# Gates beside the convolution's tanh in one visit of tables, two preparation steps a state up to the ninth, and sums of states from the fourth on

## The chip, the cores and the metric

The kernel runs on one core of a Trainium2 chip. The metric is the device time of one execution in microseconds (us). "Before" is the kernel as it stands; "after" has the change.

The core's engines are named as the profile names them: PE (TensorE, matrix products), DVE (VectorE), ACT (ScalarE, activation functions from a loaded table), POOL (GpSimd) and SP (SyncE, which here issues DMAs). PEld is TensorE's weight load.

## The reference

The input `x` is 8 batches of 256 tokens with 128 features. Three blocks follow each other, each with a residual and a layernorm: a state-space block (the one that is changed), a cross-attention to a context, and six layers of local attention with a feed-forward network. The state-space block, cut to what matters:

```python
Xn      = layernorm(X) * ln_g + ln_b
X_main  = silu(causal_depthwise_conv(Xn @ W_up1.T, taps=4) + conv_b)   # 256 channels
pp      = X_main @ W_ll.T + b_ll
delta   = softplus(pp[..., :256]);  Bm = pp[..., 256:272];  Cm = pp[..., 272:288]
A       = -exp(A_log)                                     # 256 channels x 16 states
dA      = delta[..., None] * A
A_bar   = exp(dA)
U       = X_main[..., None] * (A_bar - 1) / dA * (delta[..., None] * Bm[:, :, None, :])
H_t     = A_bar_t * H_{t-1} + U_t                         # a scan over the 256 tokens
Y_t     = sum over the 16 states of C_t * H_t
out     = X + (Y * silu(Xn @ W_up2.T)) @ W_down.T + b_down
x       = layernorm(x + out)
```

## The kernel before

**Stages.** The state-space stage takes the first 374 us of some 2310, then come cross-attention and the six layers. The stage works on four pairs of batches, `p` = 0 to 3. A tile is 128 partitions (channels or features) by 512 columns (the 256 tokens of two batches). The 256 channels are two halves, `h` = 0 and 1.

**Three generators per pair.** `pre(p)` prepares a pair: it loads and transposes `x`, makes the layernorm (`xn`), the convolution as four matmuls a half (L370, tile `conv`), then silu of it as half x times (1 + tanh) (`xm`: a tanh and an Identity on ACT, L94 and L383, a multiplication on DVE). From `xm` a matmul makes B and C (`bc_ps`, L389), which ACT copies to `bc` and stores in DRAM (L398). `minus_bc` makes `cb`, the product of B and C. `step_of` and `softplus` make `dt`, the step, for each half: an Abs, a Relu (`z`, L418, one buffer), an exp, an Ln, and an addition (on POOL for pairs 1 to 3, L424). At last the gate: two matmuls (`g_ps`), a tanh each (`gate`, L94), and a multiplication on DVE (L467).

`scan(p)` (L525) walks the 16 states. For each state SP issues two DMAs that spread a row of B and a row of C over 128 partitions (`rows`, four buffers), and for each half, a "half-state":

- `wz` = `xm` x a constant x row of B, on DVE (L538), a ring of four tiles;
- `dw`, its difference between neighbouring tokens, on POOL (L544);
- `ab` = exp(`dt` x A), on ACT (L94 `ab`), in PSUM;
- `m`, two scans over 256 tokens, on DVE (L519);
- `mc` = `m` x row of C, on POOL (L521), six buffers;
- `add_up()`: PE adds `mc` to the sum `y[h]` in PSUM with the identity as weights (L499).

`ab`, `m` and `mc` of a half-state are issued two half-states behind its `dw`. At state 2 a small product `s_ps` (L552) and a first matmul (L555) start the two sums. `add_up()` is called at the beginning of a state, from the fifth on (`n > 3`); each call adds the `mc` that have been issued since the last, so the first call adds those of the first three states (with the lag of two half-states).

`post(p)` multiplies the sum by the gate (L478), projects it down (`dn_ps`, L483), and makes the residual and its layernorm.

**How they are interleaved.** While `scan(p)` runs, `both` alternates steps of `post(p-1)` and `pre(p+1)`; each `yield` ends a step. The number of steps a state is set at L556: none at the first state, then two up to `n <= 5`, then one; two always in pair 3. In pair 2 a further generator, `project(0)` of the cross-attention (matmuls `pr`, L242, and a layernorm with its own Ln), is stepped once a state from `n > 5`; in pair 3 it takes the place of `pre`.

**Tables.** ACT's exp and Ln come from one set of tables, its tanh from another (which has exp too). `load_table` switches (`ACT_TABLE_LOAD`, L102) and keeps the program's order; `with_table` holds an activation behind the load that is issued last, and `behind_exps` holds it behind the exp that is issued last. In `pre` there are two visits to the tanh's set, each with a load there and a load back: one for `xm` (L378 to L386), one for the gate (L462 to L469).

**Order of the instructions.** Apart from the first eight steps of `pre(0)`, which are ordered by hand, a scheduler of the framework orders each engine's instructions in this stage within these limits. PSUM tiles with the tag "s" (convolution, `bc_ps`, `d_ps`, `g_ps`, `s_ps`, `dn_ps`, `pr` and others) share a ring of two.

Of the kernel before, what the change touches and what calls it, by code (L numbers as in the profile page):

```python
# [9 lines left out]
FP = mybir.dt.float32  # L10
AF = mybir.ActivationFunctionType
ALU = mybir.AluOpType
AX = mybir.AxisListType

P = 128
B, S, D = 8, 256, 128
NPAIR = B // 2
TP = 2 * S
# [31 lines left out]
def decoder_kernel(ctx: ExitStack, tc: tile.TileContext, a: dict, out: bass.AP):  # L50
# [14 lines left out]
    def ps_s(name):  # L65
        return banks[-1].tile([P, 512], FP, tag="s", name=name)
# [31 lines left out]
    def load_table(name="natural_log_exp_and_others"):  # L98

        late = name == "exp_and_others" and logs  # L100
        with tc.issue_after(logs[-1].ins) if late else ExitStack():
            table.append(tc.keep_in_program_order(A.preload_act_table_set(name)))  # L102
# [166 lines left out]
    with (  # L269
# [76 lines left out]
        def behind_exps():  # L346

            return tc.issue_after(exps[-1].ins) if exps else ExitStack()

        def pre(p, got, t_in=None):  # L350


            x = new_x(p)
            t_in = t_in or load_x(p)
            yield
            tp = turned_tokens(t_in)
            yield
            A.copy(x, tp)
            layernorm_tokens(t_in, on_act=p > 0)
            yield  # L360
            tp = turned_tokens(t_in)
            yield
            xn = xns[p % 2][:, :, KC - 1 :]
            A.activation(xn, two(tp), AF.Identity, bias=col("ssm_b"), scale=col("ssm_g"))
            xm, gate, dt, acc = [], [], [], []
            got.update(x=x, xm=xm, gate=gate, dt=dt)
            for h in range(2):
                acc.append(ps_s("conv"))
                for k in range(KC):
                    T.matmul(  # L370
                        acc[h], lhsT=w_tap[:, h, k, :],
                        rhs=xns[p % 2][:, :, k : k + S], start=(k == 0), stop=(k == KC - 1),
                    )
                yield

            for _ in range(2 if p else 0):
                yield
            load_table("exp_and_others")  # L378
            for h in range(2):
                m = sp.tile([P, TP], FP, tag=f"xm{h}", name="xm")  # L380
                with behind_exps():
                    with_table(A.activation, m, acc[h], AF.Tanh, bias=half_b[:, h : h + 1])
                A.activation(m, m, AF.Identity, bias=1.0)  # L383
                V.scalar_tensor_tensor(m, acc[h], half_b[:, h : h + 1], m, ALU.add, ALU.mult)
                xm.append(m)
            load_table()  # L386
            bc_ps = ps_s("bc_ps")
            for k in range(2):
                T.matmul(  # L389
                    bc_ps[: 2 * NS], lhsT=w_ll[:, k, DI:], rhs=xm[k], start=(k == 0), stop=(k == 1)  # L390
                )
            yield
            bc_sb = sp.tile([2 * NS, TP], FP, name="bc", bufs=1)
            with behind_exps():
                A.activation(bc_sb, bc_ps[: 2 * NS], AF.Identity, bias=col("b_bc", 0, 2 * NS))

            bc = dp.tile([2 * NS, TP], FP, name="bc_dram")
            nc.scalar.dma_start(out=bc, in_=bc_sb)  # L398
            cb = sp.tile([NS, TP], FP, name="cb", bufs=1)
            got.update(bc=bc, cb=cb, b_ps=[])  # L400

            def step_of(h):
                d_ps = ps_s("d_ps")
                for k in range(2):
                    T.matmul(
                        d_ps, lhsT=w_ll[:, k, h * P : (h + 1) * P], rhs=xm[k],
                        start=(k == 0), stop=(k == 1),
                    )
                return d_ps

            def softplus(h, d_ps):

                e = sp.tile([P, TP], FP, name="ez")
                with behind_exps():
                    A.activation(e, d_ps, AF.Abs, bias=col("b_dt", h))
                z = sp.tile([P, TP], FP, name="z", bufs=1)
                if p:
                    A.activation(z, d_ps, AF.Relu, bias=col("b_dt", h))  # L418
                else:
                    V.tensor_scalar(z, d_ps, col("b_dt", h), 0.0, ALU.add, ALU.max)  # L420
                with_table(A.activation, e, e, AF.Exp, scale=-1.0)
                logs.append(with_table(A.activation, e, e, AF.Ln, bias=1.0))
                t = sp.tile([P, TP], FP, tag=f"dt{h}", name="dt")
                (G if p else V).tensor_tensor(t, z, e, ALU.add)  # L424
                dt.append(t)

            def minus_bc():

                c_ps = ps_s("c_ps")
                T.matmul(  # L430
                    c_ps[:NS], lhsT=ident[: 2 * NS, NS : 2 * NS], rhs=bc_sb, start=True, stop=True
                )
                V.scalar_tensor_tensor(cb, c_ps[:NS], -1.0, bc_sb[:NS], ALU.mult, ALU.mult)

            if p:
                minus_bc()
                for h in range(2):
                    d_ps = step_of(h)
                    yield
                    softplus(h, d_ps)  # L440
                yield
            else:

                for h in range(2):
                    d_ps = step_of(h)
                    t = ps1.tile([P, TP], FP, tag="ab", name="b_ps")
                    T.matmul(
                        t, lhsT=ident[: 2 * NS, h : h + 1].to_broadcast([2 * NS, P]), rhs=bc_sb,
                        start=True, stop=True,
                    )  # L450
                    got["b_ps"].append(t)
                    softplus(h, d_ps)
                yield
                minus_bc()
            g_ps = []
            for h in range(2):
                g_ps.append(ps_s("g_ps"))
                T.matmul(
                    g_ps[h], lhsT=w_up2[:, h * P : (h + 1) * P], rhs=xn, start=True, stop=True
                )  # L460
            yield
            load_table("exp_and_others")  # L462
            for h in range(2):
                g = sp.tile([P, TP], FP, tag=f"gate{h}", name="gate")
                with behind_exps():
                    with_table(A.activation, g, g_ps[h], AF.Tanh)
                V.scalar_tensor_tensor(g, g, 1.0, g_ps[h], ALU.add, ALU.mult)  # L467
                gate.append(g)
            load_table()  # L469

        def post(p, x, gate, y):

# [18 lines left out]
        def scan(p, x, xm, gate, dt, bc, b_ps, cb, steps, spare):  # L491
# [31 lines left out]

            waiting = []
            for n in range(NS):  # L525
                if n > 3:
                    add_up()

                rows = sp.tile([P, 2, TP], FP, name="rows", bufs=4)
                early = n < len(b_ps)  # L530
                for i in range(1 if early else 0, 2):
                    r = i * NS + n
                    nc.sync.dma_start(out=rows[:, i, :], in_=bc[r : r + 1, :].to_broadcast([P, TP]))
                for h in range(2):
                    c = h * NS + n
                    w = wzs.pop(0)
                    wzs.append(w)
                    V.scalar_tensor_tensor(  # L538
                        w[:, :, 1:], two((xm if n < 2 else xp1)[h]), ia[:, c : c + 1],
                        two(b_ps[n] if early else rows[:, 0, :]),  # L540
                        ALU.mult, ALU.mult,
                    )
                    dw = sp.tile([P, TP], FP, name="dw", bufs=3)
                    G.tensor_tensor(two(dw), w[:, :, 1:], w[:, :, :S], ALU.subtract)  # L544
                    waiting.append((h, n, dw, rows))

                    if len(waiting) > 2:
                        scan_of(*waiting.pop(0))
                if n == 2:
                    for h in range(2):  # L550
                        s_ps = ps_s("s_ps")
                        T.matmul(s_ps, lhsT=iaT[:, h, :], rhs=cb, start=True, stop=True)  # L552
                        t = sp.tile([P, TP], FP, tag=f"yg{h}", name="xs1")
                        V.tensor_tensor(t, xm[h], s_ps, ALU.mult)
                        T.matmul(y[h], lhsT=ident, rhs=t, start=True, stop=False)  # L555
                for _ in range(0 if n == 0 else 2 if n <= 5 or p == NPAIR - 1 else 1):  # L556
                    next(steps, None)
                if n > 5:
                    next(spare, None)
# [702 lines left out]
```

## Time and profile before

| | |
|---|---|
| median of 3 runs | 2314.65 us (2313.25 to 2314.94) |
| the profiled execution | 2312.42 us, span 2310.3 us, mean granted TensorE clock 0.974 |
| busy over the whole span | PE 2150.0 (93%), DVE 1786.0 (77%), POOL 1646.2 (71%), ACT 1492.1 (65%) |
| end of the state-space stage | last `mc` starts at 372.48 us |
| table loads in the first 350 us | 17, 1283 ns each |
| `mc` (POOL L521), whole stage | 128, 1277 ns each; POOL idle ahead of them 39.5 us |

All times in views are microseconds from the start of the profiled span, unless marked ns. In a timeline, a row gives start, duration, engine, line, operation, and in brackets the idle time before it with what ended it. In the row of a group, the count is followed by busy time, mean duration in ns, and the idle time just before them with its releasers.

### The profile page before, as it was taken

How to read it: one execution, taken by the hardware profiler on the slowest of the kernel's cores; microseconds unless marked ns; L12 is line 12 of the kernel's file. 1: busy time of each engine (PE TensorE's matmuls, PEld its weight loads, DVE VectorE, ACT ScalarE, POOL GpSimd, SP SyncE). 2: the span in 40 equal slices, each digit the busy share in tenths (PEclk: the TensorE clock that was granted, in tenths of full speed). 3: DMA queues.
4: the chain of work that ended last, by engine and by line, in shares of the span. 5: the costliest groups of instructions: out<-in, count | busy, mean ns of one | idle time of the engine just before them, and what ended most of it. 6: DMA issues, size and time to landing. Idle time of an engine off the chain costs nothing.

```text
span 2310.3 us, 52806 instructions
## 1 busy us (share of the span) xinstructions
PE 2150.0 (93%) x20194; PEld 1339.5 (58%) x20194; DVE 1786.0 (77%) x2558; ACT 1492.1 (65%) x2505; POOL 1646.2 (71%) x1437
## 2 busy tenths in 40 slices
PE   7776888999988999999999999999999999999986
PEld 3232333444446666666666666666666666666664
DVE  6798876454558888888888888888888888888873
ACT  5544544455556776776777676777776776777664
POOL 4888876232478878777787777787877777777760
PEclk8888889999999999999999999999999999999999
DMA  4343331000213334333343334343343334333331
GB/s 139 96 106 98 95 88 39 2 4 1 86 26 56 65 59 90 69 70 60 70 81 71 69 63 88 67 73 62 63 85 71 72 61 76 62 63 61 56 66 32
DMA packets 438229, 153.84 MB, mean 67 GB/s; under 512 B 401887, under 2 KB 418141, under 8 KB 437853
## 3 DMA queue, kind: packets, MB, share of 16 engines
q1 hardware_dynamic: 437500, 150.10, 32.9%
q8 instruction: 162, 2.65, 0.5%
q14 instruction: 87, 0.70, 0.1%
q10 hardware_dynamic: 480, 0.38, 0.1%
HBM read 54.68 MB, written 1.31 MB: 24 GB/s over the span
## 4 chain that ended last, share of the span: by engine, by line
PE 33%; DVE 21%; ACT 21%; POOL 11%; issue 6%; DMA 1%; POOLq 0%; ACTq 0%; SPq 0%; DVEq 0%
DVE rb L700 5%; DVE qk L699 4%; PE qk_ps L682 4%; ACT sq L705 4%; ACT kz L751 3%; POOL pw L800 3%; PE f_ps L919 3%; POOL qk L703 3%; ACT pw L94 3%; PE qkT_ps L738 3%; PE o_ps L833 2%; DVE ss L712 2%; PE pr L242 2%; PE y_ps L852 2%; PE v_ps L682 2%
## 5 line engine op out<-in xcount | busy, mean ns | idle before, releaser
L703 POOL TENSOR_TENSOR qk<-qk,rb 128x512 f32<-128x512 f32 x384 | 484.7, 1284 | 108.5 <-DVE rb L700 88.7
L731 POOL TENSOR_TENSOR qk<-qk,rn 128x1024 f32<-128x1024 f32 x192 | 366.7, 1910 | 133.9 <-ACT rn L94 109.4
L682 PE MATMUL qk_ps<-wqkv,xs 128*128 128x512 f32 x768 | 364.7, 597 | 2.7 <-ACT sq L705 2.6
L705 ACT ACTIVATE sq<-qk_ps 128x1024 f32<-128x1024 f32 x192 | 196.8, 1025 | 180.5 <-DVE rb L700 170.5
L699 DVE TENSOR_TENSOR qk<-qk_ps,tab 128x1024 f32<-128x1024 f32 x192 | 233.3, 1215 | 79.9 <-PE qk_ps L682 79.1
L800 POOL TENSOR_TENSOR pw<-pw,mx 128x512 f32<-128x512 f32 x192 | 200.5, 1044 | 91.8 <-DVE mx L799 87.1
L712 DVE TENSOR_REDUCE ss<-sq 128x16 f32<-128x1024 f32 x192 | 232.5, 1211 | 40.2 <-ACT sq L705 37.4
L700 DVE TENSOR_TENSOR rb<-qk_ps,tab 128x1024 f32<-128x1024 f32 x192 | 233.2, 1214 | 0.0
L738 PE MATMUL qkT_ps<-ident,qk 128*128 128x128 f32 x1536 | 209.0, 279 | 16.1 <-ACT v L725 10.7
L94 ACT ACTIVATE pw<-pw 128x512 f32<-128x512 f32 x192 | 120.6, 628 | 155.9 <-POOL pw L800 155.6
L751 ACT COPY kz<-qkT_ps 64x1024 f32<-64x1024 f32 x192 | 193.1, 1006 | 34.5 <-PE qkT_ps L738 32.8
L833 PE MATMUL o_ps<-vz,pT 128*32 128x128 f32 x6144 | 207.5, 276 | 8.2 <-ACT pT L825 8.2
L814 POOL TENSOR_TENSOR pw<-pw,mx 128x512 f32<-128x512 f32 x192 | 200.9, 1047 | 19.5 <-DVE mx L813 17.9
L812 DVE TENSOR_REDUCE mx<-pw 128x8 f32<-128x512 f32 x192 | 130.6, 680 | 106.2 <-ACT pw L94 105.8
L852 PEld LDWEIGHTS y_ps<-oT,wo 128*128 128x128 f32 x1536 | 186.3, 192 | 44.7 <-issue 36.8
L833 PEld LDWEIGHTS o_ps<-vz,pT 128*32 128x32 f32 x6144 | 156.0, 109 | 91.8 <-ACT rn L94 35.6
L1085 POOL TENSOR_TENSOR ws<-w 128x512 f32<-128x512 f32 x64 | 81.4, 1272 | 175.3 <-ACT w L94 162.6
L786 PE MATMUL s_ps<-kz,qT 128*32 128x128 f32 x6144 | 203.0, 273 | 0.0
L682 PE MATMUL v_ps<-wqkv,xs 128*128 128x512 f32 x384 | 185.3, 605 | 16.6 <-ACT kz L751 16.6
L738 PEld LDWEIGHTS qkT_ps<-ident,qk 128*128 128x128 f32 x1536 | 164.9, 141 | 56.3 <-issue 44.2
L521 POOL TENSOR_TENSOR mc<-m,rows 128x512 f32<-128x512 f32 x128 | 162.9, 1277 | 39.5 <-PE y L499 19.8
L682 PEld LDWEIGHTS qk_ps<-wqkv,xs 128*128 128x128 f32 x768 | 131.3, 191 | 97.9 <-issue 92.7
(186 smaller groups left out, 4224.4 us busy)
## 6 DMA issues: line engine op xcount, KB each, us to landing
vz<-v SPq DMA_DIRECT2D x1152, 64.0 KB, 2.2
rows<-bc_dram SPq DMA_DIRECT2D x126, 256.0 KB, 3.8
vz<-v SPq DMA_DIRECT2D x576, 32.0 KB, 2.3
wqkv<-in_L_ffn_Wqkv SPq DMA_DIRECT2D x18, 512.0 KB, 4.3
wo<-in_L_ffn_Wo SPq DMA_DIRECT2D x48, 64.0 KB, 2.1
w<-in_L_ffn_W SPq DMA_DIRECT2D x6, 341.0 KB, 3.5
t_in<-in_x SPq DMA_DIRECT2D x4, 256.0 KB, 3.6
wkv<-in_L_xattn_Wkv SPq DMA_DIRECT2D x1, 1024.0 KB, 7.8
```

What stands on the lines that cost most here:

```text
L682: T.matmul(pr[:, i * 512 : (i + 1) * 512], lhsT=got[n]["xs"][:, tb * P : (tb + 1) * P], rhs=thirds[seq[n][0], c][:, i * 512 : (i + 1) * 51 ...
L699: V.tensor_tensor(t, p3, cs, ALU.mult)
L700: V.tensor_tensor(rb, p3, sn, ALU.mult)
L703: G.tensor_tensor(t[:, :, o], t[:, :, o], rb[:, :, f], ALU.add)
L705: A.activation(sq, p3, AF.Square)
L712: V.tensor_reduce(got[n]["ss"][:, 2 * c + tb, :], got[n]["sq"], AX.X, ALU.add)
L731: G.tensor_tensor(t, t, r, ALU.mult)
L738: T.transpose(t_ps[:, hb * P : (hb + 1) * P], t[:, 2 * hb : 2 * hb + 2, :].rearrange("p h d -> p (h d)"), ident,)
L751: A.copy(fixed3["kzs"][0][r, :, e, W + tb * P : W + (tb + 1) * P], t3[r])
L800: G.tensor_tensor(pw, pw, mx[:, 0].unsqueeze(3).to_broadcast(shape), ALU.subtract)
L833: T.matmul(o_ps[i * W : (i + 1) * W, j * P : (j + 1) * P], lhsT=pT[:, j, i * W : (i + 1) * W], rhs=vz[:, j, i].rearrange("p e d -> p (e d) ...
L852: T.matmul(y_ps[:, :P], lhsT=wts[d][0][:, hb, :], rhs=got[n]["oT", wh][:, hb, :], start=(hb == 0), stop=(hb == NHB - 1),)
```

## The change

For pairs 1 to 3 the load back after the convolution's tanh is left out; the gate's matmuls, tanh and multiplications follow `bc` within the same visit, ahead of `minus_bc`, the steps and softplus, and one load back ends it. For pair 0 the order stays. The sums are issued from the fourth state on (`n > 2`) in place of the fifth. Two steps a state are taken up to `n <= 8` in place of `n <= 5`.

```diff
                 xm.append(m)
-            load_table()
+            if not p:
+                load_table()
             bc_ps = ps_s("bc_ps")
...
             got.update(bc=bc, cb=cb, b_ps=[])
+
+            def gates():
+                g_ps = []
+                for h in range(2):
+                    g_ps.append(ps_s("g_ps"))
+                    T.matmul(
+                        g_ps[h], lhsT=w_up2[:, h * P : (h + 1) * P], rhs=xn, start=True, stop=True
+                    )
+                yield
+                if not p:
+                    load_table("exp_and_others")
+                for h in range(2):
+                    g = sp.tile([P, TP], FP, tag=f"gate{h}", name="gate")
+                    with behind_exps():
+                        with_table(A.activation, g, g_ps[h], AF.Tanh)
+                    V.scalar_tensor_tensor(g, g, 1.0, g_ps[h], ALU.add, ALU.mult)
+                    gate.append(g)
+                load_table()
...
             if p:
+                yield from gates()
                 minus_bc()
                 for h in range(2):
                     d_ps = step_of(h)
                     yield
                     softplus(h, d_ps)
                 yield
             else:
...
                 minus_bc()
-            g_ps = []
...
-            load_table()
+                yield from gates()
...
             for n in range(NS):
-                if n > 3:
+                if n > 2:
                     add_up()
...
-                for _ in range(0 if n == 0 else 2 if n <= 5 or p == NPAIR - 1 else 1):
+                for _ in range(0 if n == 0 else 2 if n <= 8 or p == NPAIR - 1 else 1):
                     next(steps, None)
```

More of the change, by code (lines that the diff above doesn't have):

```diff
@@ L454, in pre @@
                 minus_bc()
-            g_ps = []
[L456 to L468, printed above, removed]
-            load_table()
+                yield from gates()
         def post(p, x, gate, y):
```

## The prediction

> **What bounds the kernel now.** I read first the forty slices, because the change touches only the state-space stage (the first 375 of 2310 us, six and a half slices), then busy time by stretch, one stretch for each pair of batches.
>
> In the slices, GpSimd (POOL) is as full as the others over the first seven:
>
> ```profile
> PE   7776888999988999999999999999999999999986
> POOL 4888876232478878777787777787877777777760
> ```
>
> The stretches (pairs 0 to 3; columns: length, then busy time of PE, PEld, DVE, ACT, POOL, granted clock, DMA share, GB/s):
>
> ```profile
> 25.00:112.00 87.00, 68.99 (x127) 23.97 (x126) 71.22 (x117) 46.89 (x72) 73.17 (x65) 0.81 0.41 106
> 112.00:207.00 95.00, 69.11 (x143) 26.17 (x142) 81.02 (x138) 43.79 (x68) 82.57 (x72) 0.82 0.38 101
> 207.00:292.00 85.00, 68.68 (x158) 28.68 (x158) 75.32 (x120) 46.06 (x74) 73.83 (x65) 0.87 0.39 99
> 292.00:374.00 82.00, 61.79 (x127) 23.39 (x128) 59.87 (x96) 33.31 (x54) 68.81 (x63) 0.90 0.35 83
> ```
>
> POOL leads in every pair and ACT, whose tables the change regroups, is at half. So the ruler is POOL: a half-state costs it one `dw` (about 1.0) and one `mc` (about 1.23), back to back 2.23 us (see 64.36, 66.59, 68.81 below). A change gains only by the gaps between those. I number half-states 1 to 128, 32 a pair. POOL's long gaps, from the timeline (start, us, ..., idle before and releaser):
>
> ```profile
> 64.36 1.26 POOL L521 TENSOR_TENSOR mc<-m,rows 128x512 f32<-128x512 f32 x1 [8.29 <-PE y L499]
> 66.59 1.26 POOL L521 TENSOR_TENSOR mc<-m,rows 128x512 f32<-128x512 f32 x1
> 68.81 1.27 POOL L521 TENSOR_TENSOR mc<-m,rows 128x512 f32<-128x512 f32 x1
> ...
> 160.54 1.28 POOL L521 TENSOR_TENSOR mc<-m,rows 128x512 f32<-128x512 f32 x1 [3.70 <-PE bc_ps L389]
> 190.69 1.27 POOL L521 TENSOR_TENSOR mc<-m,rows 128x512 f32<-128x512 f32 x1 [5.40 <-PE s_ps L552]
> 245.78 1.27 POOL L521 TENSOR_TENSOR mc<-m,rows 128x512 f32<-128x512 f32 x1 [0.95 <-PE y L499]
> 276.86 1.27 POOL L521 TENSOR_TENSOR mc<-m,rows 128x512 f32<-128x512 f32 x1 [6.02 <-issue]
> 315.15 2.49 POOL L521 TENSOR_TENSOR mc<-m,rows 128x512 f32<-128x512 f32 x2 [6.36 <-PE y L499]
> ```
>
> 64.36 and 160.54 are visits to the other tables for the convolution's tanh; 190.69 and 276.86 are the separate gate visits of pairs 1 and 2; 315.15 is a wait for the sums on TensorE. The chain of waits confirms the last two (start, us, piece):
>
> ```profile
> 270.43 1.01 ACT gate L94 x2
> 271.47 1.28 ACT L102
> 272.76 1.31 ACT ab L94 x2
> ...
> 309.54 1.90 PE pr L242 x4
> 311.44 0.86 PE ln_mu L113 x2
> 312.30 1.91 PE pr L242 x4
> 314.20 0.87 PE y L499 x2
> 315.15 1.28 POOL mc L521
> ```
>
> Where the stage ends (last `mc` at 372.48, stage 2's first PE work at 374.85 right behind) moves the kernel one to one; after it both kernels issue the same order on every engine. The profiled run took 2312.42 (span 2310.3), 2.23 below the median of 2314.65. I work in its clock and add the difference to the median.
>
> **Pair 0 (preparing pair 1).** The built queues of the changed kernel hold 14 table loads in this stage against 18: two fewer in each of the preparations of pairs 1 and 2. The gate's two matmuls and two tanh now sit before the load back, so the first visit is longer. The load moves ahead of half-states' exps 11 and 12. Exp 10 ends at 49.2; load 1.28, exp 0.69, `xn` 0.78 give 52.0 (50.05 before); two convolutions, 16 passes at 0.43, 58.9; tanh 0.69, identity 0.63, `xm` 0.74: 61.1 (rounded up for starts); `bc_ps` 1.9: 63.0; two sums 1.7: 64.7; `g_ps` 1.7: 66.4; tanh 0.69: 67.1; load 1.28: 68.4; exp 0.69, scan 1.25: `mc` 13 at 70.4 against 68.81, **+1.6**. The second visit that goes (80 to 84.5) has no POOL gap beside it and gives nothing. The first sum, a state earlier, gives −0.2.
>
> **Pair 1.** `xm` of the second half stays at 158.2, set by VectorE's order (`wz` and statistics). `bc_ps` ends 160.3, `g_ps` 162.1, the second tanh 162.8 (the first hides under the second matmul), load 164.1; the two gate multiplies and `cb` (0.68, 0.68, 0.67) hold VectorE to 165.4, scan 1.25: `mc` 49 at 166.65 against 160.54, +6.1. Ten half-states and two `dt` later (10 x 2.23 + 2 x 1.23 = 24.8) `mc` 59 starts at 191.5 against 190.69, since the gate's 5.40 gap is gone: **+0.8**. The 1.04 wait for sums at 137.57 goes: **−1.0**.
>
> **Pair 2.** The same chain moves `mc` 81 from 245.78 to 251.8. To `mc` 91: 10 x 2.23 + 2 x 1.25 = 24.8, and two terms that before lay in the 6.02 gap. The steps come two a state, so both `dt` stand in POOL's queue together; the second waits for ACT's `z`, which waits for the single buffer that the first `dt` frees (before, 263.91 to 269.58 between them, with other work between). I take 2.5, between 0 and the 5.67 − 1.25 = 4.4 of that pair. And VectorE's `la` (3.10 us at 268.29) with statistics stands between scans: 1.8, between 0 and 3.1. So 280.9 against 276.86: **+4.0** (from −0.3 to +7.2). The wait for sums, 0.45, goes: **−0.5**.
>
> Here also lies the cost against the change: the Ln of stage 2's layernorm falls between the two loads of this visit, so the built queue has three loads (3 x 1.28 = 3.85 us) in front of exps 79 and 80. I cost them at nothing: `mc` 79, at 242.3 before, waits for the visit and has some 3 us of `dw` ahead of it. Cover gone, it is +3.6. The Trainium skill, "ScalarE: Activation LUTs", section "Table sets: the hidden batching unit", asks to batch by set and says that the back end puts a load before any activation missing from the active set: that is this case, and by it the merge is void for pair 3's preparation.
>
> A load costs what the groups give:
>
> ```profile
> L102 ACT ACT_TABLE_LOAD x17 | 21.8, 1283 | 2.1 <-issue 1.8
> ```
>
> and the tanh at 150.08 starts 0.01 after the load of 148.79 ends, so I charge 1.28 and no drain: four fewer are 5.1 us of an engine at half load. The same page, section "What ACT_TABLE_LOAD costs", adds a drain of about 1.38 to a switch; by it four loads would be about 10.6, an estimate that the trace does not bear out.
>
> **Pair 3.** The sums now come from the fourth state on, and in PE's built queue the first four stand right behind `dn_ps` and two `pr`, ahead of `ln_mu` and the other `pr` that 315.15 waited for. The first sum ends near 310.7. POOL, 4.7 late by the terms above, gets to `mc` 103 at 315.15 − 6.36 − 1.29 (the waits of 0.52 and 0.77 for `wz` at 305 to 308, hidden when POOL is late) + 4.7 = 312.2, so it waits no more: 6.36 + 1.29 + 0.22 right behind, and 0.74 at 328.53, also a wait for sums: **−8.6**. Bounds: 6.36 alone if the `wz` waits come back, nothing if the projections queued behind hold PE's ring of two accumulators.
>
> The other moves (`x` loads of the next pair two row loads later in SP's queue, `minus_bc` behind the gates) cost nothing: `rows` land in a median 3.8 us with four buffers, and `cb` is first needed at the next pair's third state. SP's cover gone, it would be one transfer of 256 KB, 3.6 us, once.
>
> **Sum:** +1.6 − 0.2 + 0.8 − 1.0 + 4.0 − 0.5 − 8.6 = −3.9. Profiled 2312.42 goes to 2308.5, the median 2314.65 to **2310.8**. A measurement of this kernel can tell about 0.2% (4.6 us) from no change: faster is below 2310.0, slower above 2319.3.
>
> **Rivals.** *Faster:* pair 2's two new waits (2.5 + 1.8) are covered, or the rest of pair 3's idle time after 327 (0.16 + 1.09 + 1.44 + 1.01 + 0.50 = 4.2) goes too: −3.9 − 4.3 = −8.2, 2306.5. For: POOL's queue in pair 2 has `dw`s between. Against: `dt` 1 did wait before. *Slower:* pair 3's gain is not kept. PE's projections `pr` and `pv`, pushed behind the sums, take the places of the ring of two late, and the sums that free the buffers for `mc` 109 come as late as the old ones; the whole 8.6 is lost, +4.7, 2319.4, and with the three loads of pair 2 uncovered 2323. It decides if the sum of half-state 103 (326.54 before) starts later than 331. Against: PE was idle 3.56 at 324.67. *The change does not do what it says:* pair 3's preparation keeps its four loads and even gains two in front of exps, so no visit is saved there. Loads are not the ruler, so this alone costs nothing; with pair 2 at its upper bound of +7.2 in place of +4.0 the sum is −0.7, 2314.0, no change.
>
> **How the numbers follow.** My forecast (2308 to 2314 as its own range) 0.5, of which a quarter falls below 2310.0; the faster rival 0.22; the slower 0.2; the third 0.08. Faster 0.35, same 0.45, slower 0.20. The range runs from the faster rival less the noise between runs (2314.94 − 2313.25 = 1.7) and 0.8, a third of the +2.4 of pairs 0 and 1, 2304, to between the slower rival's two prices, 2321.
>
> **What would show it.** Right: in pairs 1 and 2 one long POOL gap near 10 us where `mc` 49 and 81 were, none at the gates; `mc` 103 without a gap; 14 loads before 375; `dt` 1 of pair 2 waiting about 2.5. Wrong: `mc` 81 later than 253, `mc` 103 waiting for `y` again, or any difference behind the end of the stage.

## The result

| | before | after |
|---|---|---|
| median of 5 runs | 2314.65 us (2313.12 to 2315.50) | 2324.30 us (2321.37 to 2326.49) |
| ratio | | 1.0041, interval 1.0026 to 1.0056 |
| the profiled execution | 2312.42 us, span 2310.3 | 2324.30 us, span 2322.1 |
| last `mc` of the state-space stage starts at | 372.48 | 383.41 |
| from there to the end of the span | 1937.8 | 1938.7 |

The change made the kernel slower by 9.65 us. All but a microsecond of the 11.8 us between the two spans lies in the state-space stage: its last `mc` comes 10.93 later, and what follows takes the same time.

Line numbers after L399 are shifted by up to 20 in the changed kernel: `mc` is L527, `dw` L550, `wz` L544, the sums L505, `dt` L443, the scans L525. The stretches of the changed kernel, one for each pair (length; then busy time of PE, PEld, DVE, ACT, POOL; granted clock, DMA share, GB/s):

```profile
25.00:118.00 93.00, 71.95 (x126) 23.65 (x126) 71.89 (x118) 43.99 (x70) 72.68 (x65) 0.80 0.41 99
118.00:216.00 98.00, 71.32 (x142) 26.44 (x140) 78.94 (x133) 40.39 (x65) 81.37 (x71) 0.81 0.38 97
216.00:308.00 92.00, 70.53 (x161) 30.36 (x162) 72.09 (x116) 47.39 (x77) 74.95 (x66) 0.87 0.40 93
308.00:386.00 78.00, 62.49 (x129) 23.03 (x129) 62.48 (x106) 32.25 (x53) 69.56 (x63) 0.89 0.37 86
```

POOL's busy time is that of before, 298.6 against 298.4 us over the four; the first three stretches are longer and the last is shorter. So the time is idle time of POOL. Summing the holes between POOL's rows from the first `mc` to the last gives 47.8 us before and 58.8 after, a difference of 11.0; the last `mc` is 10.9 late (the first one starts 0.5 early). By pair (half-states 1, 33, 65, 97 to the next) the holes went from 11.9 to 18.2, from 11.7 to 16.3, from 11.2 to 17.0 and from 13.0 to 7.2.

The largest of them, from POOL's timeline of the changed kernel (start, us, ..., idle before and releaser):

```profile
74.77 1.26 POOL L527 TENSOR_TENSOR mc<-m,rows 128x512 f32<-128x512 f32 x1 [15.60 <-PE d_ps L424]
163.05 2.49 POOL L527 TENSOR_TENSOR mc<-m,rows 128x512 f32<-128x512 f32 x2 [2.27 <-PE y L505]
173.99 1.27 POOL L527 TENSOR_TENSOR mc<-m,rows 128x512 f32<-128x512 f32 x1 [8.44 <-PE d_ps L424]
266.01 1.27 POOL L527 TENSOR_TENSOR mc<-m,rows 128x512 f32<-128x512 f32 x1 [8.73 <-PE d_ps L424]
276.39 1.27 POOL L443 TENSOR_TENSOR dt<-z,ez 128x512 f32<-128x512 f32 x1 [2.44 <-ACT ez L94]
326.08 1.27 POOL L527 TENSOR_TENSOR mc<-m,rows 128x512 f32<-128x512 f32 x1 [2.38 <-PE y L505]
```

The gate's gaps of 5.40 and 6.02 are gone, as intended. But pair 0, where the gate's visit had cost POOL nothing, now has one gap of 15.60 in place of 8.29, and pair 2, where the convolution's visit had hardly shown on POOL (0.95), has 8.73. In pair 3 the gap of 6.36 ahead of `mc` 103 is 2.38. The chain of waits ahead of 266.01 says what stands inside a merged visit (start, us, piece):

```profile
253.85 3.43 PE y L505 x8
257.28 1.83 PE bc_ps L390 x4
259.11 1.92 PE g_ps L407 x4
261.03 1.72 PE y L505 x4
262.74 0.96 PE c_ps L449 x2
263.70 1.93 PE d_ps L424 x4
```

A count is of passes, and each product here takes two: the 128 sums of the stage are 256 rows, so x8 is four sums and x4 two. Only the two `g_ps` products are needed before ACT can load back; four sums and `bc_ps` stand in front of them. `c_ps` is in the chain because VectorE makes `cb` ahead of the waiting scan; `d_ps` is named as the releaser, but the waiting scan doesn't read it: releasers are inferred. Table loads fell as read from the queues, and a load cost the same:

```profile
L102 ACT ACT_TABLE_LOAD x11 | 14.1, 1283 | 2.0 <-issue 1.8
```

(the window to 360 us; two more, charged to the Ln's line, stand at 244.28 and 245.89).

### The profile page after: what moved, and what is told of

Read it like the earlier page. It is cut to its first block, busy times and chain, and to the rows that moved or that the text cites. A ratio compares the mean times of both kernels' runs of the same rounds, so it can differ in the third digit from the quotient of the medians.

```text
span 2322.1 us, 52820 instructions
## 1 busy us (share of the span) xinstructions
PE 2155.9 (93%) x20194; PEld 1340.5 (58%) x20194; DVE 1782.8 (77%) x2558; ACT 1485.3 (64%) x2501; POOL 1645.8 (71%) x1437
## 4 chain that ended last, share of the span: by engine, by line
PE 32%; DVE 21%; ACT 20%; POOL 12%; issue 6%; DMA 0%; POOLq 0%; ACTq 0%; SPq 0%; DVEq 0%
DVE rb L706 5%; DVE qk L705 4%; PE qk_ps L688 4%; ACT sq L711 4%; POOL pw L806 3%; ACT kz L757 3%; POOL qk L709 3%; PE f_ps L925 3%; ACT pw L94 3%; PE qkT_ps L744 2%; DVE ss L718 2%; PE o_ps L839 2%; PE y_ps L858 2%; PE s_ps L1082 2%; DVE mx L818 2%
## 5 line engine op out<-in xcount | busy, mean ns | idle before, releaser
L527 POOL TENSOR_TENSOR mc<-m,rows 128x512 f32<-128x512 f32 x128 | 164.9, 1294 | 46.0 <-PE d_ps L424 32.8
L505 PE MATMUL y<-mc,ident 128*128 128x512 f32 x256 | 150.8, 704 | 44.4 <-POOL mc L527 43.1
```

## The experiments

For each kernel I give the lengths of the four pairs against before, from the profiles, and the medians against before's of the same set of runs.

| kernel | pair 0 | pair 1 | pair 2 | pair 3 | median | ratio (interval) |
|---|---|---|---|---|---|---|
| after (all three parts) | +6.1 | +4.1 | +6.8 | −5.6 | +9.7 | 1.0041 (1.0026 to 1.0056) |
| e_merge | +4.4 | +1.7 | +7.0 | −0.2 | +12.2 | 1.0049 (1.0036 to 1.0062) |
| e_steps | +4.0 | +3.8 | +7.3 | −6.2 | +7.9 | 1.0031 (1.0020 to 1.0042) |
| e_sums | 0.0 | +1.1 | 0.0 | +1.6 | +1.8 | 1.0009 (1.0001 to 1.0018) |
| e_merge_sums | +4.3 | +2.7 | +7.3 | +2.8 | +14.3 | 1.0056 (1.0043 to 1.0069) |
| e_merge_steps | +6.2 | +1.6 | +4.6 | −5.9 | +6.8 | 1.0032 (1.0020 to 1.0045) |
| x_split | +4.3 | +3.8 | +5.3 | −5.9 | +7.7 | 1.0035 (1.0023 to 1.0048) |
| x_gate_first | +1.0 | +5.5 | +7.3 | −5.7 | +9.2 | 1.0038 (1.0026 to 1.0051) |
| x_gate_conv | +4.3 | +3.8 | +5.9 | −7.3 | +7.9 | 1.0037 (1.0024 to 1.0051) |
| x_split_before | −0.7 | −2.6 | 0.0 | +0.7 | −1.5 | 0.9992 (0.9984 to 1.0001) |
| y_gf_old | +2.7 | +0.7 | +3.1 | −2.2 | +3.8 | 1.0020 (1.0011 to 1.0029) |
| y_gf_old_split | −1.8 | −0.6 | +4.3 | −2.3 | −1.7 | 0.9994 (0.9985 to 1.0003) |
| y_ms_late | +2.4 | +1.8 | +4.9 | −2.2 | +7.4 | 1.0033 (1.0023 to 1.0044) |
| s_p2 | −0.5 | −0.4 | +3.9 | −5.9 | −1.5 | 0.9994 (0.9985 to 1.0003) |
| w1 | −2.7 | −3.2 | −0.6 | +1.7 | −2.5 | 0.9988 (0.9979 to 0.9997) |
| w2 | −2.3 | −3.2 | +4.3 | −6.1 | −6.6 | 0.9967 (0.9954 to 0.9979) |

### The three parts alone and in twos

**e_merge**, only the merge:

```diff
 after.py
-                if n > 2:
+                if n > 3:
                     add_up()
...
-                for _ in range(0 if n == 0 else 2 if n <= 8 or p == NPAIR - 1 else 1):
+                for _ in range(0 if n == 0 else 2 if n <= 5 or p == NPAIR - 1 else 1):
```

> Only the merge of the two visits; sums from the fifth state and steps up to n <= 5 as before. Theory V (the merged visit is the loss: between the last convolution tanh and the load back stand bc_ps, the sums, g_ps and the gate's tanh, and almost no exp): the gaps of POOL in the visits stay near those of after, 15 us in pair 0, 8 to 10 in pairs 1 and 2, the gate gaps of 5.4 and 6.0 go, and the wait for the first sums of pair 3 (6.4) stays; 12 to 17 us slower than before, 2327 to 2331. Rival S (two steps a state leave no exps inside the visit, so steps and merge are bad together only): the visit holds two or more exps per pair again, gaps under 6 us in pairs 1 and 2; within 4 us of before.

Measured: 2326.36, 12.2 us slower. Theory V's side in time, and S falls: the merge loses in full at the old steps. But "almost no exp" was wrong: each of the three merged visits holds four exps here, against two in the changed kernel, and still `mc` 15 of pair 0 waits 12.02. In pairs 1 and 2 the long waits are 7.96 and 10.51, and pair 3 keeps its wait (6.57).

**e_steps**, only the steps:

```diff
 before.py
-                for _ in range(0 if n == 0 else 2 if n <= 5 or p == NPAIR - 1 else 1):
+                for _ in range(0 if n == 0 else 2 if n <= 8 or p == NPAIR - 1 else 1):
```

> Only two steps a state up to n <= 8. Theory V: the two visits stay apart, the steps only bring the second one nearer; within 3 us of before, 2312 to 2318. Rival S: alone it also costs little, since the loss needs both; the same. If the earlier Ln work brings in the two extra loads of pair 2 or both additions for dt wait for one another, +3 to +5.

Measured: 2322.06, 7.9 us slower, which neither theory gave. With two steps a state the gate's visit follows the convolution's more closely: pair 0 now has a second gap, 5.01 at 84.34, six half-states behind the first, where before had none. My reading is that POOL has no work left over by then. And pair 3 is 6.2 shorter, without any change to the sums.

**e_sums**, only the sums:

```diff
 before.py
-                if n > 3:
+                if n > 2:
                     add_up()
```

> Only sums from the fourth state on. Both theories: the waits for sums at half-states 39, 71 and 103 go (1.0, 0.5 and 6 to 7 us); 5 to 8 us faster than before, 2306.5 to 2309.5. If the gain of pair 3 in the changed kernel came only from its being late, 2 us or less.

Measured: 2315.97, 1.8 us slower; both theories were wrong, and so was the prediction. Pair 3 is longer by 1.6, and the wait at half-state 103 fell only from 6.36 to 4.58, which later waits for scans took back. Pair 1 lost too. VectorE's and PE's timelines of pair 1 show how, first of e_sums, then of before:

```profile
141.52 0.66 DVE L117 TENSOR_TENSOR ln_xc<-r,ln_mu 128x512 f32<-128x512 f32 x1
142.99 1.86 PE L135 MATMUL ln_var<-mean_w,ln_sq 128*128 128x1 f32 x8 [4.93 <-ACT ln_sq L119]
145.60 3.62 PE L499 MATMUL y<-mc,ident 128*128 128x512 f32 x4
```

```profile
137.16 0.66 DVE L117 TENSOR_TENSOR ln_xc<-r,ln_mu 128x512 f32<-128x512 f32 x1
141.86 0.95 PE L135 MATMUL ln_var<-mean_w,ln_sq 128*128 128x1 f32 x8
143.14 1.88 PE L499 MATMUL y<-mc,ident 128*128 128x512 f32 x4
```

In PE's queue `ln_var` of the previous pair's layernorm has six sums ahead of it and two behind it in both kernels. What moved is VectorE's `ln_xc`, from which ACT makes the square `ln_sq`: it is ordered 4.4 us later, behind more scans. PE stands for it (4.93 in e_sums, 4.63 in the changed kernel). Behind that wait PE is slow: `ln_var` and the two sums take about twice their time, and the profile's granted clock from 143 to 149 is 0.50, where before has 1.00 from 141 to 147. So the convolution starts 3.8 later (150.16 against 146.36), some 2.9 of it by the slow passes, the next sums come behind it, and `mc` 47 waits 2.27 for them in e_sums, e_merge_sums and the changed kernel alike.

**e_merge_sums** and **e_merge_steps**, two parts each (the edits above):

> Merge and sums, steps as before. Theory V: the merge's loss less the sums' gain, 6 to 10 us slower than before, near after's 2324. Rival S: 2 to 8 us faster than before.

> Merge and steps, sums from the fifth state as before. If the sums are worth nothing (as alone, and with the merge), 2322 to 2326, and pair 3 as short as in the changed kernel (75 us from half-state 97 to 128), since the steps alone gave it 6 us. If the sums are what removes the wait at half-state 103, pair 3 takes 80 us and the kernel 2329 or more.

Measured: 2328.49 and 2319.93. Merge and sums lose more than theory V's 6 to 10. Without the sums the changed kernel loses 6.8 rather than 9.7, and pair 3 stays as short (−5.9): the sums lose in each company that was run, 1.8 alone, 2.1 with the merge and 2.9 with both. The last two are within the intervals of the medians, but the profiles agree: the stage ends 4.1 and 4.9 later with them. Steps and sums without the merge were not run. Pair 3's gain belongs to the steps. The parts do not add: alone they lose 12.2, 7.9 and 1.8, together 9.7. The lengths differ from the sum of the parts in pairs 0 to 2, and the likely reason is that the second gap which the steps uncover (5.01 in pair 0) belongs to the visit that the merge removes.

### What makes the merged visit long

**x_split**, rows of B and C in tiles of their own:

```diff
 after.py
-                rows = sp.tile([P, 2, TP], FP, name="rows", bufs=4)
+                rows = sp.tile([P, TP], FP, name="rowc", bufs=4)
+                rowb = sp.tile([P, TP], FP, name="rowb", bufs=4)
...
-                    nc.sync.dma_start(out=rows[:, i, :], in_=bc[r : r + 1, :].to_broadcast([P, TP]))
+                    nc.sync.dma_start(
+                        out=rows if i else rowb, in_=bc[r : r + 1, :].to_broadcast([P, TP])
+                    )
...
-                        two(b_ps[n] if early else rows[:, 0, :]),
+                        two(b_ps[n] if early else rowb),
...
-                G.tensor_tensor(mc, m, rows[:, 1, :], ALU.mult)
+                G.tensor_tensor(mc, m, rows, ALU.mult)
```

It was tried because VectorE's timeline of the changed kernel in pair 0's visit reads:

```profile
61.95 0.75 DVE L544 SCALAR_TENSOR_TENSOR wz<-xm_ps,ia,rows 128x512 f32<-128x512 f32 x1 [2.07 <-DMA rows<-bc_dram]
...
63.55 0.72 DVE L384 SCALAR_TENSOR_TENSOR xm<-conv,half_b,xm 128x512 f32<-128x512 f32 x1
...
72.55 0.68 DVE L452 SCALAR_TENSOR_TENSOR cb<-c_ps,bc 16x512 f32<-16x512 f32 x1 [0.50 <-PE c_ps L449]
73.37 2.42 DVE L525 TENSOR_TENSOR_SCAN m<-dw,ab 128x256 f32<-128x256 f32 x4
```

The second `xm` stands behind a `wz` whose row of B shares a tile with a row of C that only an `mc` frees: the last `mc` before the visit ends at 58.17, and its successor lands at 61.95.

> The changed kernel with the two rows of a state in tiles of their own (rowb, rowc, four buffers each, the same memory), so that the row of B is free when wz has read it, and no longer waits for the mc of four states before. Theory R (in the visit, VectorE stands in front of the second xm at a wz whose row waits for the last mc before the visit: 58.17 + 3.78 = 61.95 in pair 0): the wait of wz goes, the second xm of pair 0 starts near 60.4 in place of 63.55 and the gap before half-state 13 falls by about 3; the refill after the visits of pairs 1 and 2 (4.75 and 7.16 at half-states 52 and 84) loses 1 to 2.5 each; 4 to 8 us faster than the changed kernel, 2316 to 2320. Rival (the row's wait is covered by the convolution and by the tanh): within 1.5 us of the changed kernel's 2324.3.

Measured: 2320.90, a loss of 7.7 us where the changed kernel's is 9.7, so 1.9 by the medians (3.5 by the stage's end in the two profiles), short of the 4 to 8. The gap in pair 0 fell from 15.60 to 12.00 as theory R said, but not the way it said: the `wz` now waits for POOL's `dw`, which frees its place in the ring, and the second `xm` starts at 63.00, only 0.55 earlier.

```profile
60.55 0.75 DVE L547 SCALAR_TENSOR_TENSOR wz<-xm_ps,ia,rowb 128x512 f32<-128x512 f32 x1 [1.48 <-POOL dw L553]
```

POOL stops 1.34 later, behind the same 12 `mc`, and `mc` 13 comes 2.25 earlier. The other 1.7 of this are PE's pace. The two sums and the gate's two products behind `bc_ps` are, in the changed kernel and in x_split:

```profile
65.30 3.40 PE L505 MATMUL y<-mc,ident 128*128 128x512 f32 x4
68.50 2.20 PE L407 MATMUL g_ps<-xn,w_up 128*128 128x512 f32 x4
```

```profile
64.75 1.98 PE L505 MATMUL y<-mc,ident 128*128 128x512 f32 x4
66.57 1.88 PE L407 MATMUL g_ps<-xn,w_up 128*128 128x512 f32 x4
```

In the changed kernel passes start up to 0.85 us apart, in x_split 0.43, and the granted clock from 64 to 68 is 0.71 against 1.00. PE had been idle 3.25 ahead of `bc_ps` in the former and 0.71 at most in the latter. POOL lost 0.88 again at 81.33: pair 0 is 1.7 shorter.

**x_gate_first**, the gate ahead of `bc_ps`:

```diff
 after.py
             if not p:
                 load_table()
+            else:
+                yield from gates()
             bc_ps = ps_s("bc_ps")
...
             if p:
-                yield from gates()
                 minus_bc()
```

(`gates` is defined above it.)

> The changed kernel with the gate's matmuls, tanh and the load back ahead of bc_ps, which they don't need; steps and sums as in the changed kernel. Theory Q (the visit is long by what is queued between the last convolution tanh and the load back: bc_ps on PE, its copy on ACT, cb in front of the scan on VectorE): the gaps at half-states 13, 49 and 81 shrink by 2 to 3.5 us each, 6 to 10 us faster than the changed kernel, 2314 to 2318. Rival (the gate's own matmuls, tanh and multiplications are what lengthens the visit): under 3 us faster.

Measured: 2322.37, by the medians 0.5 us less than the changed kernel's loss; the rival's side in the total. By pair the theory is half right: pair 0 lost 5.1 us of its delay, to 10.36 for the gap. Not all of that is the shorter chain: PE's passes start 0.43 apart in this visit and the granted clock from 64 to 68 is 1.00, which in x_split was worth 1.7. Pairs 1 and 2 became worse, with one gap of 14.03 and 14.71. ACT's timeline in pair 1 shows a second cause:

```profile
146.52 1.28 ACT L102 ACT_TABLE_LOAD   x1
152.98 0.69 ACT L94 ACTIVATE xm<-conv,half_b 128x512 f32<-128x512 f32 x1 [5.18 <-PE conv L370]
```

The visit opens ahead of the convolution and waits 5.18 for it, and no exp is ordered between the load and the load back. What exps inside a visit are worth is not shown: the short visits of before hold none, those of e_merge hold four each, and it loses 12.2.

**x_gate_conv**, the gate's matmuls and tanh ahead of the convolution:

```diff
 after.py
+            if p:
+                yield from gates()
             for h in range(2):
                 acc.append(ps_s("conv"))
...
-            for _ in range(2 if p else 0):
+            for _ in range(1 if p else 0):
                 yield
-            load_table("exp_and_others")
+            if not p:
+                load_table("exp_and_others")
```

(here `gates` loads the tables and makes both tanh, without a load back; that follows `xm`, as in pair 0).

> The changed kernel with the gate's matmuls and tanh ahead of the convolution: one visit of load, two gate tanh, two convolution tanh, load back, the gate's tanh lying where ACT waits for the convolution. Theory Q: the visit is as long as that of before but for the two gate matmuls ahead of the convolution (1.7 us); gaps of 9 to 11 in pair 0, 4 to 7 in pairs 1 and 2, none at the gates; 8 to 14 us faster than the changed kernel, 2310 to 2316. Rival: under 3 us faster, because the convolution now waits for both gates to leave the ring of two accumulators.

Measured: 2321.03, 7.9 us slower than before and 1.8 less than the changed kernel's loss; theory Q's 8 to 14 us did not come, the rival's "under 3" did. Pairs 1 and 2 have two gaps each, 7.34 and 6.87, 6.34 and 6.34. As the rival said, the convolution waits for the ring: in pair 1 its first pass starts at 154.27, released by the multiplication of the first gate, 4.6 behind the start of `ln_bc`, where before has 1.0.

**y_gf_old**, the gate ahead of `bc_ps` with the steps and sums of before, **y_ms_late**, e_merge_steps with a later opening, and the rows split on both sides:

```diff
 y_ms_late: e_merge_steps with
-            for _ in range(2 if p else 0):
+            for _ in range(4 if p else 0):
                 yield
```

> Merge with the gate ahead of bc_ps, with the steps and sums of before. Theory O (a merged visit is cheap if it opens late, with the convolution done, and closes early, with the gate ahead of bc_ps): the gaps of pairs 0 to 2 are 9 to 11, 5 to 7 and 5 to 7, the gate's gaps are gone; 3 us faster to 3 us slower than before, 2310 to 2316. Rival (any merge loses, as the merge alone did with 12 us): 2320 or more.

> Merge and steps, sums as before (2320 so far), with four empty steps in place of two between the convolution and the visit. Theory O: the visit no longer opens ahead of the convolution (ACT's wait for conv of 3 to 5 us goes) and has two exps inside; 3 to 6 us less, 2314 to 2317. Rival (only the chain behind the last tanh counts, bc_ps, g_ps, gates): within 1.5 us of 2320.

> The kernel before with the rows of B and C in tiles of their own. Theory R (VectorE stands at a wz whose row waits for an mc, in front of xm): it gained 3.4 us in the changed kernel, so 2 to 4 us here too, 2310 to 2312. Rival (the row's wait costs only in the longer visit of the changed kernel): within 1.5 us of before.

> The same with the rows of B and C in tiles of their own: 2 to 4 us less than with the shared tile, 2307 to 2313 under theory O; the rival 2317 or more.

Measured: y_gf_old 2316.86, against e_merge's 12.2 us of loss only 3.8. At the old steps the place of the gate is worth 8.4 us (by the profiles 1.7, 1.0, 3.9 and 2.0 in the four pairs): the rival's 2320 falls, though theory O's 2316 was just missed and the merge still loses. y_ms_late 2320.48, as e_merge_steps: its rival holds. Opening later gained 3.8 in pair 0 and lost 3.7 in pair 3. x_split_before 2311.62 and y_gf_old_split 2311.44: neither can be told from before, although pair 1 of the former is 2.6 shorter in its profile. The rows' tile is worth 5.4 us in the merged visit (2316.86 to 2311.44). By the profiles pair 0 has 4.5 of it, and there too PE's pace differs: the granted clock behind the first gate product is 0.50 from 69 to 74 in y_gf_old, 1.00 from 60 to 68 with tiles of their own.

### Where pair 3's gain comes from, and a faster kernel

**s_p2**, **w1** and **w2**:

```diff
 s_p2: before.py with
-                for _ in range(0 if n == 0 else 2 if n <= 5 or p == NPAIR - 1 else 1):
+                for _ in range(
+                    0 if n == 0 else 2 if n <= (8 if p == 2 else 5) or p == NPAIR - 1 else 1
+                ):
 w1: x_split_before with, for the preparation of pair 1 alone, the gate ahead of bc_ps in one visit
-            load_table()
+            if p == 1:
+                yield from gates()
+            else:
+                load_table()
             bc_ps = ps_s("bc_ps")
 w2: w1 with the steps of s_p2
```

> The kernel before with two steps a state up to n <= 8 in pair 2 alone. Theory P (an early end of the preparation in pair 2 moves the projections' copies qT ahead of an exp of pair 3, so the first sums of pair 3 come 6 us earlier; the same steps push the two visits of pair 2 together and cost it 7): pairs 0 and 1 as before, pair 2 +7, pair 3 -6, together within 2 us of before, 2312 to 2316. Rival (pair 3 gains only because pairs 0 and 1 are late): pair 3 as before, 2319 or more.

> The kernel before with the rows of B and C in tiles of their own, and the merged visit, gate ahead of bc_ps, only where it gained: in the preparation of pair 1. By the stretches measured, pair 0 -1.8, pair 1 -2.6, pairs 2 and 3 within 1 of before: 3 to 4.5 us faster than before, 2308.5 to 2310. Rival (the gains were those of separate kernels and don't add): 2311.5, as each alone.

> w1 with two steps a state up to n <= 8 in pair 2 alone. Theory P: +7 in pair 2 and -6 in pair 3 against w1, so within 2 us of w1. Rival (with rows of their own the visits of pair 2 no longer lose by it): 4 to 6 us faster than w1, 2303 to 2306.

Measured: s_p2 2312.63. Pairs 0 and 1 keep their time, pair 3 is 5.9 shorter, so the rival falls: the gain comes from pair 2's steps. They cost pair 2 3.9, not 7. The mechanism inside theory P was wrong in a detail: the copies `qT` stand where they stood. PE's timeline of s_p2 shows the order that changed:

```profile
308.05 2.07 PE L242 MATMUL pr<-cn,wkv 128*128 128x512 f32 x4
309.95 1.02 PE L499 MATMUL y<-mc,ident 128*128 128x512 f32 x2
310.81 1.02 PE L113 MATMUL ln_mu<-r,mean_w 128*128 128x512 f32 x2
```

Before, `ln_mu` and four more passes of `pr` stood between those `pr` and the first sum, which started at 314.04. Now the first sum is at 309.95, and the gap ahead of `mc` 103 is 1.09.

w1 is 2311.61, 2.5 us below before, a little under its 3 to 4.5; part of it went into pair 3 (+1.7). Against x_split_before the merge for pair 1 alone is worth 2.0 in pair 0's profile, and can't be told in the medians. w2 is 2307.53, ratio 0.9967 (0.9954 to 0.9979), 4.1 below w1: theory P's "within 2 us" falls, and the rival has its time but not its reason, since pair 2 still loses 4.9 against w1, while pair 3 gains 7.8. By the ends of the stage the gains add: s_p2 3.2 and w1 5.1 earlier than before, w2 7.7. w2 is faster than before by 6.6 us and than the changed kernel by some 16. Its gap in pair 0 is 6.78, that of the gate in pair 1 3.45.

## Why the prediction was wrong

What held: POOL is the ruler, and its idle time accounts for the delay; the stage's end passes on one to one; the merge lengthens the first visit and removes the gaps of the gate; the loads are not the ruler; the second `dt` of pair 2 waits (2.44, I took 2.5); pair 3 gains at the first sums. Two of the signs that I had named for being wrong came: `mc` 81 stands at 266.01, and `mc` 103 waits for `y` (2.38). The errors of the four pairs, 4.7, 4.3, 3.3 and 3.0, less the 0.5 by which the first `mc` is early, are the 14.8 between the −3.9 forecast and the 10.9 measured at the stage's end.

- **Pair 0, forecast +1.4, measured +6.1.** The failed step is the chain of the visit, in two terms. I let the second `xm` end at 61.1; it ended at 64.27, because VectorE reaches it only behind a `wz` that waits for a row (61.95). And I charged every pass of PE 0.43: behind PE's idle time of 3.25 the two sums took 3.2 where I had 1.7, and `g_ps` 0.5 more than the 1.7 that I gave it. The stretches in the prediction show a mean granted clock of 0.81 for this pair before the change, and my chain held no slow pass. With `bc_ps`, half of which was done by then (−0.9), this is the 4.4 by which `mc` 13 came later than my 70.4 (74.77). The load's 1.28 and the tanh's 0.60 were as charged. `cb` is not in the way here: the scan starts at 73.37, 0.03 behind its exp.
- **Pair 1, forecast −0.2, measured +4.1.** The −1.0 for the sums is the step that failed. The wait at half-state 40 did go, but in company of merge and steps the sums cost 2.5 here (4.1 against 1.6 in e_merge_steps), through VectorE's late `ln_xc` and PE's slow passes behind it. The rest is the chain: PE was still at four sums (161.95 to 165.47) when the second `xm` was done, which put `mc` 49 9.7 behind the end of that `xm` (164.3 to 173.99), where I had 8.45. My 8.45 was itself 0.6 too long by its own rows: 162.8 and three multiplications, or 164.1 and an exp, give 164.8 and not 165.4.
- **Pair 2, forecast +3.5, measured +6.8.** The failed step is the same chain: counted from the start of the pair `mc` 81 came 10.6 later and not 6.0. The visit's gap (8.73) is that of pair 1, with four sums ahead of `bc_ps`, and the sums cost 2.2 (6.8 against 4.6), again with a wait for `ln_sq` (4.32) and a granted clock of 0.50 behind it, from 242 to 246. The three loads ahead of exps 79 and 80 were hidden as I had argued: without the sums the step from `mc` 78 to 79 is 6.60, against 7.05 before, although e_merge_steps has those loads. In the changed kernel the step is 8.72, but exp 79 ends at 247.87 and its scan starts at 249.96, behind other work of VectorE that had waited for PE's `ln_bc`.
- **Pair 3, forecast −8.6, measured −5.6.** The mechanism was right, its cause was not: I gave it to the sums, but it is the work of the steps in pair 2 (s_p2 −5.9, e_sums +1.6). The size was off because I held PE's first sum near 310.7 while I let POOL be late; PE's chain was late with it, and 2.38 of the wait stayed.
- **The rivals.** The slower one had nearly the right time for the wrong reason: pair 3 kept most of its gain, the loss was in pairs 0 to 2. The largest term was the merge itself, +12.2 alone, for which I had +1.6, +0.8 and +4.0.

The Trainium skill ("ScalarE: Activation LUTs", "Table sets: the hidden batching unit") says that the back end puts a load before every activation that needs one, and the trace agrees: two loads stand at the Ln, at 244.28 and 245.89. The same section's rule to batch by table set is not borne out in time here: fewer loads came with a merge that lost 12.2 us alone. The drain that the same page adds to a load ("What ACT_TABLE_LOAD costs") did not show in after either: the exp at 72.65 starts 0.02 after the load of 71.35 ends.

What stays open: why the scheduler puts four exps inside a visit at some settings, two or none at others, and why it moves `ln_xc`; the queues show that it does, not why. PE's slow passes are read from traces, and no run changes the clock alone. An idle time of PE does not always bring them: x_gate_first has one of 3.37 in the same visit and a clock of 1.00 behind it. Whether the rows' wait could be taken away with a fifth buffer was not tried.

## What to carry to other kernels

Price a visit to another table by what no instruction of the ruling engine may pass: everything queued on PE, VectorE and ACT between the load there and the load back, row by row in each queue, not by its loads. Look also at the granted clock behind long idle times of PE: here its passes took twice their time in some of these stretches. Before merging two visits, see whether the second one showed on the ruling engine at all (here it did not in pair 0), and put what the second needs ahead of what it doesn't. A kernel ordered by a scheduler answers an edit in places that the edit doesn't touch: try each part alone and read the lengths by stage, since a part that gains in one stage can carry one that loses.

## What was unexpected

Starting sums a state earlier, which adds no work, cost 1.8 us alone and 2.9 in company (2324.30 against 2319.93, each less its own before), because VectorE's `ln_xc` was ordered 4.4 us later; PE stood 4.9 us for what depends on it (alone; 4.6 in company) and was slow behind that. Two tiles in place of one, of the same size, were worth 1.9 us in the changed kernel, 5.4 in y_gf_old and nothing that can be told in the kernel before.
